# Four layers on a graph of 2048 nodes: adjacency loaded later, products ahead of the degrees, one-hot columns on ScalarE, 1/degree applied in the mixing

## The chip, the cores and the metric

The kernel runs on one core of a Trainium2 chip. Its engines are TensorE (PE: matmuls, with its weight loads listed apart as PEld), VectorE (DVE), ScalarE (ACT), GpSimd (POOL) and SyncE (SP, which only issues transfers here). Each engine works through its own queue in order; transfers are issued from the queues of SP, ACT and POOL. The metric is the device time of one execution in microseconds (us). A trace is one profiled execution; its span is counted from the first to the last instruction.

## The reference, cut to what matters

`x` is 8 x 2048 x 64, `adj` is 2048 x 2048 of zeros and ones with a full diagonal, `H` is 2048 x 64 (node by hyperedge). Four layers follow each other, each `x = layernorm(x + layer(x))`. The change touches layer 0:

```
h = x @ W                                    # 8 x 2048 x 64
alpha = softmax over the nodes of a hyperedge of leaky_relu(h @ a_node)
agg = alpha @ h                              # 8 x 64 hyperedges x 64
all_he[n, e] = elu(beta * h[n] + (1 - beta) * agg[e]),  beta = sigmoid(h[n] @ a_gn + agg[e] @ a_ge)
g[n] = sum over the hyperedges e of node n of softmax(scores of e) * all_he[n, e]
deg = max(sum of a row of adj, 1)
industry = (adj / deg) @ (x @ W_ind)
out = softmax-weighted mix of industry and g, by tanh(f @ fcW + fcb) @ av
```

Layers 1 to 3 are products with `adj` (layer 1 with 1/sqrt(deg + 1) on both sides), a Chebyshev convolution with node-wise weights, and three rounds of a small network on [v, adj @ v].

## The kernel before

The batch is worked in NP = 4 pairs (two batch entries of 64 features make 128 partitions). The nodes are NT = 16 tiles of 128 rows or NCH = 4 chunks of 512 columns; JT = 4 tiles make a chunk. The transposed adjacency stays in SBUF for the whole kernel as 16 tiles of 128 x 2048, 1 MB each, in a type with which a 128 x 512 matmul is fast; to keep precision every left operand is split into a high and a low part (`split`, L163), so that a product has two matmuls per tile and chunk. The names `ug`, `du`, `ph` and `pcm` are PSUM tiles that share one tag `ph` with two buffers of two banks.

The stages that the change touches, in order of time:

- **The loop over h** (L505 to L550), one iteration per node tile t. PE makes h for the four pairs (`ph`), DVE and ACT make a row block `st` of 584 columns per node (exponentials, (h+1) times e^gn, and the slot numbers of the node's hyperedges), which ACT's queue stores to `hs_hbm` (L538); PE also adds up `pagg`, the sums over the nodes of each hyperedge. `st` has four buffers. Adjacency tiles are loaded from POOL's queue by `load_adj` (L209): five ahead of the loop, each after a copy that waits for an x tile (`load_adj_after`, L395), ten more in the loop as `paced` says (L401), the last one after it. SP loads `xt` tiles four iterations ahead and, for the products, `xc` chunks, of which `parts` makes high and low parts (the low ones on POOL).
- **Hyperedges** (L572 to L639). `filler` is a generator of matmuls that `fill(n)` (L327) draws from: `products()` (L271). It first gives the 64 degree matmuls `du` (ones times an adjacency tile, 16 tiles x 4 chunks), then for each pair p and half g (two chunks of 512) the 64 matmuls of adj @ x in `ug`. Between the small steps of the hyperedge scores come fill(24), fill(14), fill(10) and fill(24): 72 of the 576 matmuls. From the degrees come `dinv` (for layer 1) and, by transposes, `inv` rows of 1/deg over all partitions, inside the first half. Each `ug` is multiplied by `inv` on DVE (L324) and stored to `u0_hbm` by SP.
- **The slot loop** (L693 to L724). The nodes are sorted by their number of hyperedges, so that tile t of the sorted order has 12, 5, 5, 4, 4, 4, 3, 3, 3, 3, 2, 2, 2, 2, 2, 1 slots (57 in all): slot s of a node is its s-th hyperedge. `fetch_rows` (L231) gathers the rows of a tile from `hs_hbm` by an indirect transfer on POOL's queue. `slots` (L241) makes from the slot numbers one-hot matrices `o`, 128 x 128, one per slot: by `is_equal`, on DVE for 8 of the first tile's and on POOL for the other 49. `begin` (L670) makes the high and low parts of a row block, and the coefficients R and co from the matmuls `ps` of o. For each slot PE adds three matmuls into `pz` (rows of h twice, and o times the hyperedge table), DVE multiplies by R, ACT takes the exponential into `y`, DVE makes the elu and multiplies by co, and POOL adds up `acc`. `pz` has three buffers, `y` two. Every slot draws fill(6), every tile but the last fill(3). The sums are scattered to `gs_hbm` from POOL's queue.
- **The mixing steps** (L867 to L891), 16 of them (pair by chunk), pipelined over two steps, with fills of eight matmuls in four places. `mix_parts` loads g and `u0_hbm`, multiplies by W_ind (`pi`) and copies the result into `ind`; `mix_scores`, `mix_weigh` and `mix_end` make the scores, the mix and the layernorm. The rest of `products()` is drawn in steps 0 to 4; from then on the filler is layer 1 (`layer1`, L830), whose operands `l1_parts` are made in step 4.

Matmuls and transposes made by `mm` and `transpose` (L172, L175) keep the order of the program, as do the adjacency loads and gathers on POOL and, for pair 0, the parts. A scheduler puts the other instructions into each engine's queue. Adjacency tile t and the parts' chunk t // 4 are needed by four matmuls in a half.

Of the kernel before, what the change touches and what calls it, by code (L numbers as in the profile page):

```python
# [37 lines left out]
ALU = mybir.AluOpType  # L38
# [18 lines left out]
def tile_gnn_fast(  # L57
# [47 lines left out]
    def cols(c, n=C):  # L105
        return slice(c * n, (c + 1) * n)
# [105 lines left out]


# [6 lines left out]
    x2_hbm = [dram.tile([P, NT, P], F32, name=f"x2_hbm{p}") for p in range(NP - 1)]  # L220
    gs_hbm = dram.tile([N, BF], F32, name="gs_hbm")
# [19 lines left out]
    def slots(t, psum, tag, bufs):  # L241

        pt = psum.tile([E, P], F32, tag=tag, name="pslot", bufs=bufs)
        transpose(pt, hrows[t][:, BF + 8:])
        slot = hy.tile([P, P], BF16, tag="slot", name="slot", bufs=2)
        for i in range(2):
            nc.scalar.copy(slot[i * E:(i + 1) * E, :], pt)
        one_hot[t] = []
        for s in range(sum(n > t for n in SLOT_TILES)):
            o = hrp.tile([P, P], F32R, tag="o", name="o", bufs=17)  # L250
            eng = nc.vector if t == 0 and s % 3 < 2 else nc.gpsimd
            made = eng.tensor_scalar(o, slot, float(s + 1), None, op0=ALU.is_equal)
            if t == 0:
                tc.keep_in_program_order(made)
            one_hot[t].append(o)
# [15 lines left out]
    def products():  # L271


        du = [pph.tile([P, 2, C], F32, tag="ph", name=f"du{g}", bufs=2) for g in range(2)]
        for t in range(NT):
            for c in range(NCH):
                mm(du[c // 2][:, c % 2, :], lhsT=ones_r, rhs=adj[t][:, cols(c)], start=t == 0, stop=t == NT - 1)
                yield
        for c in range(NCH):
            r = slice(c * P // NCH, (c + 1) * P // NCH)  # L280
            evacuate(deg4[r, :], du[c // 2][r, c % 2, :])
        deg1 = hy.tile([P, NT], F32, name="deg1")
        inv = []
        for p in range(NP):
            for g in range(2):
                own = (2 * g, 2 * g + 1)
                ug = pph.tile([P, 2, C], F32, tag="ph", name="ug", bufs=2)
                u = {c: ug[:, c % 2, :] for c in own}
                for t in range(NT):
                    for i in range(2):  # L290
                        for c in own:
                            mm(
                                u[c], lhsT=part[t // JT][i][:, t % JT, :], rhs=adj[t][:, cols(c)],
                                start=t == 0 and i == 0, stop=t == NT - 1 and i == 1,
                            )
# [7 lines left out]
                    if p == 0 and g == 0 and t == 3:  # L303

                        pdc = places["small"]([P, JT, P], "pdc")
                        for j in range(JT):
                            transpose(pdc[:, j, :], deg4[:, cols(j, P)])
                        pdc = pdc.rearrange("p j (c r) -> p c j r", c=NCH)[:, :, :, 0]
                        d1 = deg1.rearrange("p (c j) -> p c j", c=NCH)
                        nc.vector.tensor_scalar(d1, pdc, 1.0, None, op0=ALU.add)  # L310
                        nc.gpsimd.tensor_tensor(dinv, deg1, neg_half[:, :NT], ALU.pow)
                        nc.vector.tensor_scalar(d1, pdc, 1.0, None, op0=ALU.max)
                        nc.vector.reciprocal(deg1, deg1)
                    if p == 0 and g == 0 and t in (12, 13, 14, 15):
                        c = t - 12
                        pt = places["small"]([P, C], "pinv")
                        for j in range(JT):
                            k = c * JT + j
                            transpose(pt[:, cols(j, P)], deg1[:, k:k + 1].to_broadcast([P, P]))
                        inv.append(va.tile([P, C], F32, name=f"inv{c}"))  # L320
                        nc.scalar.copy(inv[c], pt)
# [14 lines left out]
    with tc.tile_pool(name="pa_ps", bufs=1, space=PSUM) as pps:  # L336
# [233 lines left out]
        ones_r = ta.tile([P, P], F32R, name="ones_r")  # L570
        nc.vector.tensor_copy(ones_r, ones)
# [19 lines left out]
        fill(14)  # L591
# [7 lines left out]
        fill(10)  # L599
# [37 lines left out]

        fill(NT * NCH - 48 + 8)
# [26 lines left out]
    with ExitStack() as pb_scope:  # L665
# [29 lines left out]
        for t in range(NT):  # L695
            S, both, ohs, R, co = now
            acc = pl.tile([P, B, F], F32, tag="acc", name="acc", bufs=2)
            for s in range(S):
# [6 lines left out]
                fill(6)  # L705
# [4 lines left out]
                y = pl.tile([P, B, F], F32, tag="y", name="y", bufs=2)  # L710
# [34 lines left out]
    mp = mix_scope.enter_context(tc.tile_pool(name="mix", bufs=1, side="right"))  # L745
    lps_scope = ExitStack()
# [7 lines left out]
    def mix_parts(i):  # L754

        p, c = divmod(i, NCH)
        gn = mp.tile([P, JT, P], F32, tag="gn", name="gn", bufs=2)
        nc.sync.dma_start(
            gn, gs_hbm[c * C:(c + 1) * C, p * P:(p + 1) * P].rearrange("(t p) f -> p t f", p=P)
        )  # L760
        ut = mp.tile([P, C], F32, tag="ut0", name="ut0", bufs=2)
        nc.sync.dma_start(ut, u0_hbm[p][:, cols(c)])
        pi = lps.tile([P, C], F32, tag="mm", name="pi", bufs=4)
        mm(pi, lhsT=bd_ind, rhs=ut, start=True, stop=True)
        inds[i] = mp.tile([P, C], F32, tag="ind", name="ind", bufs=2)
# [100 lines left out]

    steps = NP * NCH  # L867
# [1031 lines left out]
```

## Time and profile before

| what | value |
|---|---|
| three runs | 2235.95, 2239.82, 2240.61 us, median 2239.82 |
| the profiled run | 2242.28 us, span 2240.4 us |
| busy, share of the span | PE 88%, PEld 57%, DVE 50%, POOL 22%, ACT 17% |
| mean granted TensorE clock | 0.95 |
| loop over h, first matmul `ph` to last `pagg` | 21.1 to 79.8 us |
| degrees `du`, first to last | 79.8 to 98.1 us |
| slot loop, first `ps` to last matmul of its last slot | 100.7 to 279.3 us |
| first mixing matmul `pi` | 295.2 us |
| first matmul of layer 1 | 362.0 us |
| one-hot 128 x 128 on POOL, on DVE (medians) | 556 ns, 290 ns |
| landing of a 1 MB adjacency tile, of a 292 KB h store (medians) | 8.9 us, 6.3 us |

The page gives the whole execution in 40 slices of 56 us, each digit being a busy share in tenths; the stages of the table fill the first six and a half. Matmuls are pipelined, so that the time from one to the next is shorter than the duration that the trace gives for one.

### The profile page before, as it was taken

Reading aid. Unit: us, or ns where it says so; the run is one execution under the profiler, and the core shown is the slowest. Engines: PE = TensorE matmul, PEld = TensorE weight load, DVE = VectorE, ACT = ScalarE, POOL = GpSimd, SP = SyncE. Lnnn points to the kernel's source line nnn. Section 1 sums busy time; section 2 is a strip of 40 time slices with the busy share of each in tenths; the row PEclk is TensorE's granted clock in tenths of the full one; section 3 lists DMA queues with packets and bytes.
Section 4 is the critical chain, followed back from the end, with each engine's and each line's share of the span. In section 5 each row is a group of like instructions: output and inputs, shape, how many; then the busy total and the mean of one; then the engine's idle time right before and its main releaser. Section 6 shows DMA issues by size and latency. Waiting matters only on the chain. (4 is left out here: it accounts for less than half of the span.)

```text
span 2240.4 us, 19695 instructions
## 1 busy us (share of the span) xinstructions
PE 1981.7 (88%) x7292; PEld 1282.5 (57%) x7292; DVE 1110.8 (50%) x1837; ACT 376.2 (17%) x688; POOL 501.0 (22%) x464
## 2 busy tenths in 40 slices
PE   5898879998659999799999999999986998989994
PEld 3676645665544444375455456447444776867773
DVE  4478835666432232216854763782883233332322
ACT  1233323222111111110010001001001212212110
POOL 2378823344223232200110110100010010010102
PEclk8899989999869999999999999999998999999997
DMA  9612223222210000000000000000001101111110
GB/s 310 223 47 77 101 95 114 92 96 81 101 38 0 19 19 19 26 17 5 10 5 5 8 7 3 7 9 1 7 7 36 43 24 52 38 52 43 43 34 20
DMA packets 72521, 108.50 MB, mean 48 GB/s; under 512 B 26704, under 2 KB 34928, under 8 KB 69920
## 3 DMA queue, kind: packets, MB, share of 16 engines
q1 hardware_dynamic: 61728, 72.61, 10.5%
q0 software_dynamic: 5088, 25.89, 3.4%
q10 hardware_dynamic: 5600, 8.65, 1.1%
q8 instruction: 59, 0.97, 0.2%
q14 instruction: 46, 0.38, 0.1%
HBM read 78.22 MB, written 28.90 MB: 48 GB/s over the span
## 5 line engine op out<-in xcount | busy, mean ns | idle before, releaser
L1018 PE MATMUL py<-wp,xg 128*128 128x512 f32 x1024 | 448.4, 597 | 8.5 <-DVE fcav L1023 5.8
L1018 PEld LDWEIGHTS py<-wp,xg 128*128 128x128 f32 x1024 | 193.6, 191 | 254.3 <-issue 215.3
L173 PE MATMUL u<-adj,hi 128*128 128x512 f32 x768 | 255.8, 414 | 0.0
L173 PE MATMUL u<-adj,lo 128*128 128x512 f32 x768 | 247.4, 402 | 0.0
L965 PE MATMUL u<-pt,xn 128*128 128x512 f32 x512 | 230.6, 609 | 8.3 <-DVE u L974 7.1
L1023 DVE TENSOR_TENSOR fcav<-py,emb_n 128x512 f32<-128x512 f32 x256 | 177.1, 692 | 51.7 <-PE py L1018 37.1
L1024 DVE TENSOR_REDUCE r<-fcav 128x32 f32<-128x512 f32 x256 | 175.4, 685 | 8.1
L965 PEld LDWEIGHTS u<-pt,xn 128*128 128x128 f32 x512 | 98.5, 195 | 131.9 <-issue 117.0
L652 PE MATMUL u<-adj,vh 128*128 128x512 f32 x512 | 158.9, 409 | 15.1 <-ACT vh L168 11.0
L173 PEld LDWEIGHTS u<-adj,hi 128*128 128x128 f32 x768 | 142.9, 190 | 40.9 <-issue 11.2
L1026 POOL TENSOR_TENSOR r<-r,bias 128x256 f32<-128x256 f32 x32 | 23.4, 731 | 636.4 <-DVE r L1024 636.4
L173 PEld LDWEIGHTS u<-adj,lo 128*128 128x128 f32 x768 | 144.9, 190 | 33.8
L156 POOL TENSOR_TENSOR ln_r<-ln_e,neg_half 128x8 f32<-128x8 f32 x64 | 106.5, 1663 | 215.6 <-DVE ln_e L154 209.0
L652 PE MATMUL u<-adj,vl 128*128 128x512 f32 x512 | 152.3, 399 | 0.0
L959 DVE TENSOR_SCALAR pt<-pt 128x512 f32<-128x512 f32 x64 | 48.8, 780 | 175.0 <-ACT pt L958 173.4
L1114 DVE SCALAR_TENSOR_TENSOR fcav<-fcav,ar 128x512 f32<-128x512 f32 x64 | 44.3, 693 | 175.6 <-ACT ar L1113 175.4
L652 PEld LDWEIGHTS u<-adj,vh 128*128 128x128 f32 x512 | 96.4, 190 | 45.5 <-ACT vh L168 12.5
L1096 POOL TENSOR_TENSOR r<-r,xn 128x512 f32<-128x512 f32 x16 | 20.5, 1280 | 434.1 <-DVE r L1095 434.1
L963 POOL TENSOR_TENSOR acc<-acc,pt 128x512 f32<-128x512 f32 x60 | 79.7, 1328 | 165.6 <-DVE pt L959 162.7
L652 PEld LDWEIGHTS u<-adj,vl 128*128 128x128 f32 x512 | 96.7, 189 | 22.3 <-issue 0.7
L150 ACT ACTIVATE r<-ln_c 128x512 f32<-128x512 f32 x64 | 40.4, 631 | 270.4 <-DVE ln_c L146 255.6
L144 DVE TENSOR_REDUCE ln_m<-r 128x8 f32<-128x512 f32 x64 | 43.8, 685 | 70.0 <-POOL r L1030 27.9
(340 smaller groups left out, 2737.1 us busy)
## 6 DMA issues: line engine op xcount, KB each, us to landing
adj<-in_adj_t POOLq DMA_DIRECT2D x16, 1024.0 KB, 8.9
fcav<-in_adj_t SPq DMA_DIRECT2D x64, 256.0 KB, 2.9
x_hbm<-r SPq DMA_DIRECT2D x28, 256.0 KB, 2.1
hs_hbm<-st ACTq DMA_DIRECT2D x16, 292.0 KB, 6.3
xt<-in_x_t SPq DMA_DIRECT2D x16, 256.0 KB, 6.9
xc<-in_x_n SPq DMA_DIRECT2D x16, 256.0 KB, 2.7
u_hbm<-ut SPq DMA_DIRECT2D x16, 256.0 KB, 2.4
gn<-gs_hbm SPq DMA_DIRECT2D x16, 256.0 KB, 3.5
```

Of the source, the lines that this page charges most:

```text
L144: nc.vector.tensor_reduce(mean, r, AX.X, ALU.add)
L150: nc.scalar.activation(r, xc, AF.Square)
L156: nc.gpsimd.tensor_tensor(rstd, vare, neg_half[:, :groups], ALU.pow)
L173: tc.keep_in_program_order(nc.tensor.matmul(*args, **kw))
L652: nc.tensor.matmul(u[c], lhsT=half[:, j, :], rhs=adj[t][:, cols(c)], start=t == 0 and i == 0, stop=ends and not own,)
L959: nc.vector.tensor_scalar(pt, pt, 1.0, None, op0=ALU.max)
L963: nc.gpsimd.tensor_tensor(acc, acc, pt, ALU.add)
L965: nc.tensor.matmul(u[p], lhsT=xn[p][:, t, :], rhs=pt, start=t == 0, stop=t == NT - 1)
L1018: nc.tensor.matmul(py.rearrange("p o d -> p (o d)"), lhsT=xg[b][:, q, cols(j, P)], rhs=wp[:, q, cols(k)], start=q == 0, stop=q == 1,)
L1023: nc.vector.tensor_tensor(pr, py, e_b, ALU.mult)
L1024: nc.vector.tensor_reduce(r[:, j, b, cols(k, OH)], pr, AX.X, ALU.add)
L1114: nc.vector.scalar_tensor_tensor(a, a, 1.0, ar.bitcast(F32), op0=ALU.mult, op1=ALU.not_equal, accum_out=left[:, t, k:k + 1],)
```

## The change

- Three adjacency tiles instead of five are loaded ahead of the loop over h, five instead of ten in it (`paced`), and eight after it: one at once, and seven behind the gathers of the first two row blocks and the parts of the last two chunks.
- `products()` begins with the first half of pair 0; the 64 degree matmuls come after that half, two chunks at a time (`degrees`). What follows from the degrees (`inverses`) is spread over the second half of pair 0. ones_r is made at the start.
- The fills between the hyperedge steps are 10, 8, 8 and 6; each slot draws 7; 36 are drawn between the slot loop and the mixing. `y` has three buffers.
- The one-hots of the first tile are all made by DVE; the other 45 by ACT, in two activations: far = |slot - (s+1)|, o = relu(1 - far). The column `number` holds -(s+1).
- `ug` is copied by ACT without the factor 1/deg. The `inv` rows go to a buffer `inv_hbm` in memory, are loaded as one tile `inv_row` of 128 x 2048 when the mixing begins, and multiply `pi` where it was copied.

```diff
+    ones_r = hy.tile([P, P], F32R, name="ones_r")
+    nc.vector.tensor_copy(ones_r, ones)
+    number = hy.tile([P, 12], F32, name="number")
+    for i in range(12):
+        nc.gpsimd.memset(number[:, i:i + 1], -1.0 - i)
...
+    inv_hbm = dram.tile([P, N], F32, name="inv_hbm")
...
-            eng = nc.vector if t == 0 and s % 3 < 2 else nc.gpsimd
-            made = eng.tensor_scalar(o, slot, float(s + 1), None, op0=ALU.is_equal)
             if t == 0:
-                tc.keep_in_program_order(made)
+                tc.keep_in_program_order(
+                    nc.vector.tensor_scalar(o, slot, float(s + 1), None, op0=ALU.is_equal)
+                )
+            else:
+
+                far = hy.tile([P, P], BF16, tag="far", name="far", bufs=2)
+                nc.scalar.activation(far, slot, AF.Abs, bias=number[:, s:s + 1])
+                nc.scalar.activation(o, far, AF.Relu, bias=1.0, scale=-1.0)
...
-        du = [pph.tile([P, 2, C], F32, tag="ph", name=f"du{g}", bufs=2) for g in range(2)]
...
+        def degrees(g):
+            du = pph.tile([P, 2, C], F32, tag="ph", name=f"du{g}", bufs=2)
+            for t in range(NT):
+                for i in range(2):
+                    mm(
+                        du[:, i, :], lhsT=ones_r, rhs=adj[t][:, cols(2 * g + i)], start=t == 0, stop=t == NT - 1
+                    )
+                    yield
...
+                row = va.tile([P, C], F32, tag="ut", name="inv", bufs=2)
+                nc.scalar.copy(row, pt)
+                nc.sync.dma_start(inv_hbm[:, cols(c)], row)
...
+                turning = inverses() if p == 0 and g == 1 else iter(())
...
+                            if t > 1:
+                                next(turning, None)
...
-                    nc.vector.tensor_tensor(ut, u[c], inv[c], ALU.mult)
+                    nc.scalar.copy(ut, u[c])
                     nc.sync.dma_start(u0_hbm[p][:, cols(c)], ut)
+                if p == 0 and g == 0:
+                    yield from degrees(0)
+                    yield from degrees(1)
...
-        for t in range(5):
-            load_adj_after(t, xt[min(t, 3)][:, 0, 0:1])
-        paced = {1: 5, 2: 6, 4: 7, 5: 8, 7: 9, 8: 10, 10: 11, 11: 12, 13: 13, 14: 14}
+        for t in range(3):
+            load_adj_after(t, xt[t + 1][:, 0, 0:1])
+        paced = {2: 3, 5: 4, 8: 5, 11: 6, 14: 7}
...
-        load_adj(NT - 1)
+        load_adj(len(paced) + 3)
         fetch_rows(0)
         fetch_rows(1)
         for c in (2, 3):
             fetch(0, c)
             parts(0, c)
+        for t in range(len(paced) + 4, NT):
+            load_adj(t)
...
-        fill(24)
+        fill(10)
...
-        fill(14)
+        fill(8)
...
-        fill(10)
+        fill(8)
...
-        fill(NT * NCH - 48 + 8)
+        fill(6)
...
-                fill(6)
+                fill(7)
...
-                y = pl.tile([P, B, F], F32, tag="y", name="y", bufs=2)
+                y = pl.tile([P, B, F], F32, tag="y", name="y", bufs=3)
...
+    inv_row = mp.tile([P, N], F32, name="inv_row")
+    nc.scalar.dma_start(inv_row, inv_hbm[:])
...
-        nc.vector.tensor_copy(inds[i], pi)
+        nc.vector.tensor_tensor(inds[i], pi, inv_row[:, cols(c)], ALU.mult)
...
+    fill(36)
     steps = NP * NCH
```

More of the change, by code (lines that the diff above doesn't have):

```diff
@@ L271, in products, with inverses @@
     def products():
-        du = [pph.tile([P, 2, C], F32, tag="ph", name=f"du{g}", bufs=2) for g in range(2)]
-        for t in range(NT):
-            for c in range(NCH):
[L277 to L283, printed above, removed]
+        deg1 = hy.tile([P, NT], F32, name="deg1")
+        def degrees(g):
[6 more added lines that the diff above has]
+                    yield
+            for i in range(2):
+                c = 2 * g + i
+                r = slice(c * P // NCH, (c + 1) * P // NCH)
+                evacuate(deg4[r, :], du[r, i, :])
+        def inverses():
+            pdc = places["small"]([P, JT, P], "pdc")
+            for j in range(JT):
+                transpose(pdc[:, j, :], deg4[:, cols(j, P)])
+            pdc = pdc.rearrange("p j (c r) -> p c j r", c=NCH)[:, :, :, 0]
+            d1 = deg1.rearrange("p (c j) -> p c j", c=NCH)
+            nc.vector.tensor_scalar(d1, pdc, 1.0, None, op0=ALU.add)
+            nc.gpsimd.tensor_tensor(dinv, deg1, neg_half[:, :NT], ALU.pow)
+            nc.vector.tensor_scalar(d1, pdc, 1.0, None, op0=ALU.max)
+            nc.vector.reciprocal(deg1, deg1)
+            for _ in range(8):
+                yield
+            for c in range(NCH):
+                pt = places["small"]([P, C], "pinv")
+                for j in range(JT):
+                    k = c * JT + j
+                    transpose(pt[:, cols(j, P)], deg1[:, k:k + 1].to_broadcast([P, P]))
+                row = va.tile([P, C], F32, tag="ut", name="inv", bufs=2)
+                nc.scalar.copy(row, pt)
+                nc.sync.dma_start(inv_hbm[:, cols(c)], row)
+                for _ in range(4):
+                    yield
         for p in range(NP):
@@ L302, in products @@
                             fetch(p + 1, (c + 2) % NCH)
[L303 to L321, printed above, removed]
                 for c in own:
                     ut = va.tile([P, C], F32, tag="ut", name="ut", bufs=2)
-                    nc.vector.tensor_tensor(ut, u[c], inv[c], ALU.mult)
+                    nc.scalar.copy(ut, u[c])
                     nc.sync.dma_start(u0_hbm[p][:, cols(c)], ut)
+                if p == 0 and g == 0:
+                    yield from degrees(0)
+                    yield from degrees(1)
     def fill(n):
@@ L569, in tile_gnn_fast @@
         ta = ta_scope.enter_context(tc.tile_pool(name="ta", bufs=1, side="right"))
-        ones_r = ta.tile([P, P], F32R, name="ones_r")
-        nc.vector.tensor_copy(ones_r, ones)
         places["small"] = lambda shape, name: pps.tile(shape, F32, tag="sm", name=name, bufs=2)
         filler = products()
-        fill(24)
+        fill(10)
         gv = pagg[:, 0:G * (F + 1)].rearrange("p (g c) -> p g c", c=F + 1)
```

## The prediction, made before the changed kernel was run

> **What bounds the kernel now.** I read the page's slices first, to see where TensorE (PE) has gaps, then a table by stretch, then the chain of waits of the first 420 us, the groups by shape, and timelines at the joints. All sums are against the profiled span, 2240.4 us; the three other runs have a median of 2239.8.
>
> ```profile
> PE   5898879998659999799999999999986998989994
> POOL 2378823344223232200110110100010010010102
> PEclk8899989999869999999999999999998999999997
> GB/s 310 223 47 77 101 95 114 92 96 81 101 38 0 19 19 19 26 17 5 10 5 5 8 7 3 7 9 1 7 7 36 43 24 52 38 52 43 43 34 20
> ```
>
> Slices are 56 us. PE is near full after 350 us, short of it in slices 1 to 6, and the DMA engines are busy at the start. All edits but the mixing's act before 362 us, so I cut that part at its joints. The columns are PE, PEld, VectorE (DVE), ScalarE (ACT), GpSimd (POOL) busy us with counts, PE clock, DMA share, GB/s:
>
> ```profile
> 16.40:79.80 63.40, 46.44 (x244) 31.41 (x244) 35.46 (x123) 10.95 (x51) 10.15 (x23) 0.78 0.96 342
> 79.80:100.70 20.90, 19.99 (x88) 16.10 (x87) 7.83 (x27) 7.24 (x19) 8.44 (x10) 0.94 0.46 157
> 100.70:117.80 17.10, 16.05 (x72) 12.84 (x71) 8.37 (x21) 2.31 (x5) 8.98 (x9) 0.90 0.10 32
> 117.80:279.30 161.50, 138.49 (x582) 106.15 (x580) 130.83 (x225) 54.06 (x111) 137.51 (x132) 0.96 0.24 77
> 279.30:295.20 15.90, 0.00 (x0) 0.01 (x1) 5.74 (x7) 0.60 (x1) 4.35 (x4) 0.64 0.34 123
> 295.20:361.90 66.70, 63.59 (x225) 40.49 (x225) 34.64 (x47) 22.83 (x35) 17.87 (x13) 0.96 0.32 101
> ```
>
> Row 1 is the loop over h: DMA share 0.96. Row 2 is the hyperedge part with the degrees; rows 3 and 4 the slot loop (its sixth slot starts at 117.8); row 5 a hole without one matmul; row 6 the mixing steps up to layer 1's first product. In row 4 POOL (137.5), PE (138.5) and DVE (130.8) are all within 20% of 161.5: three engines coupled, POOL with the most to lose.
>
> ```profile
> ACT st L520 <- DMA hs_hbm<-st: 29.9, 9, 7.5
> PE pi L173 <- DMA ut<-u_hbm: 15.9, 1, 15.9
> PEld ps L173 <- POOL o L252: 13.6, 15, 2.9
> PE ps L173 <- POOL o L252: 10.4, 14, 2.7
> ...
> L719 POOL TENSOR_TENSOR acc<-acc,y 128x512 f32<-128x512 f32 x41 | 54.3, 1325 | 20.8 <-DVE y L718 16.8 <-DVE R L685 2.1 <-DVE R L682 0.7
> L718 DVE TENSOR_TENSOR y<-y,co 128x512 f32<-128x512 f32 x41 | 42.6, 1050 | 0.1
> L252 POOL TENSOR_SCALAR o<-slot 128x128 fp32r<-128x128 bf16 x46 | 28.9, 639 | 3.5 <-ACT slot L247 2.6
> ```
>
> The four waits name the four places: rows of h that can't leave (29.9), the hole (15.9), one-hots that come late from POOL (10.4 on PE; the 13.6 of the weight loads is largely the same time). The groups show what POOL does there.
>
> ```profile
> 113.84 0.39 PE L173 MATMUL pz<-hrh,ident_r 128*128 128x512 f32 x1
> 115.92 0.39 PE L173 MATMUL pz<-hrh,ident_r 128*128 128x512 f32 x1
> ...
> 349.32 1.02 PE L173 MATMUL pi<-ut,bd_ind 128*128 128x512 f32 x2
> 357.35 1.02 PE L173 MATMUL pi<-ut,bd_ind 128*128 128x512 f32 x2
> ```
>
> An undisturbed slot of 3+6 matmuls takes 2.08 us, 0.23 each. A mixing step that has only five product matmuls left takes 8.0 us; one with 32 takes 14.3 (320.7 to 335.0).
>
> **What the Trainium skill says.** "DMA: Bandwidth & Descriptors", section "Issuing engines are not separate DMA queues": transfers from ACT, SP and GpSimd run on the same 16 engines and interleave. The trace agrees: the 292 KB h stores, on another queue than adjacency, take 6.3 us (median) while 1 MB tiles pass. "GPSIMD Engine Reference", section "Key points": it shares SBUF interfaces with VectorE and collides with VectorE instructions of two SBUF inputs. The trace agrees: y*co averages 1050 ns here, and 0.68 us where POOL rests. "ScalarE: Activation LUTs", section "Table sets": relu and abs are in every set. The trace has one table load, at 11.7 us, for exp and tanh; abs and relu are not in it.
>
> **The change, part by part.** PE work is moved, not removed: 64 degree and 512 product matmuls stay. The fills before the slot loop fall from 72 to 32, those inside rise from 387 to 444, 36 come behind it, and 64 are left for the mixing instead of 117. The order on each engine below is that of the built program.
>
> 1. *The loop over h.* It moved 342 GB/s x 63.4 us = 21.7 MB. About 7.7 adjacency tiles leave it, 8.1 MB; 13.6 MB at the same rate take 40 us, so it would end at 56. Undisturbed, an iteration takes 1.8 us (38.3 to 45.6 for four); the first three, mixed with the sort, lasted to 33.8; 13 x 1.8 and the last sum give 59. Some store waits stay: I take 62 for 79.8. The twelve extra memsets on POOL at the start cost what the sixteen of `caps` do, under 0.6 us, before a transfer-bound stretch: nothing on the path.
>
> 2. *To the slot loop.* ps started 20.9 us after the loop. Now only 24+8 matmuls stand between the small steps (he, pht, tanh, pse, slots) instead of 64+8; the row gather waits for the last h store (10.1 us now; I take 5), then 2 us of issue and 3.6 to land, slot copies 0.5, twelve one-hots on DVE 2.2 (8 took 1.45). I take 14 us: ps at 76.
>
> 3. *Tiles 9 to 15.* They stand on POOL's queue behind those gathers and the low parts v2l and v3l, so issue starts about 10 us after the loop. Seven tiles of 1.05 MB at 370 GB/s (between the 342 mean and the peaks above 400) and 2 us give the last at +32. PE waits in order: pz and ps stand behind the product that needs the tile. The sixth slot starts some 14 matmuls later: 62+32+3 = 97 instead of 117.8. Gained 21, with 35 matmuls (8 us) deferred.
>
> 4. *Rest of the slot loop, 52 slots.* PE: 52x10+14x3 = 562 matmuls x 0.23 = 130, plus ps, transposes, pinv about 11: 141, at a clock of 0.97 145; the same sum for now (510) gives 134 at 0.96, so 27 of 161.5 are lost. POOL loses 45 one-hots, about 28 us, and DVE the multiply by 1/degree (12 x 0.67) and some collisions. ACT gets 45 pairs. The row for far is missing; the nearest, tanh with a column bias, takes 475 ns at 256 and 684 at 512 elements: 371 at 128; casts give 298. The skill's price (same page, "What ACT_TABLE_LOAD costs") is 387 and 293, less 93 overlap each. So 0.5 to 0.67 us a pair, 22 to 30 us, and 0.58 for each ut copy: ACT goes from 54 to about 88 of 160. In order on ACT, exponentials stand behind a batch of up to five pairs, 2.5 us; three pz and now three y buffers cover about 6 us of slots. I take the one-hot waits as gone and 14 us of the 27 as left: 159. Slot loop ends at 256 instead of 279.3: 23. The degrees' PSUM tiles share two buffers with the products; ut's copies stand behind four exponentials, with three slots of slack: no cost, at most 2.
>
> 5. *The hole* stays 16 us, but 36 matmuls (8.3) run in it, which pays for most of what was deferred.
>
> 6. *Mixing until layer 1.* Steps of 11.1, 14.3, 10.6 (16 fills), 8, 8 = 52 instead of 62: 10. Layer 1's first product waits 3.15 for v0h now; the casts stand earlier in the new order: 1 to 3 more. I take 11. The product with inv_row replaces a PSUM copy of the same shape (0.68): nothing. Its 1 MB load stands on ACT's queue and may wait for the last scatter, as gn does; it lands 7 to 9 us later, ind(0) was due about 5 after: 0 to 5 lost, I take 3; behind it on ACT only two ut copies that nobody needs yet. Four 256 KB stores of inv pass where DMA moves 77 GB/s: nothing.
>
> Sum: 23+11-3 = 31. 2240 - 31 = **2209 us**. After 362 us nothing changes.
>
> **Rivals.**
> (a) *VectorE takes over in the slot loop.* DVE is busy 130.8 of 161.5 with two SBUF inputs beside POOL's acc. If the 27 us of loss stay, the stretch takes 172: gain 31-13, 2222. Against: POOL's share falls by a fifth.
> (b) *The h loop isn't released.* If store latency, not bytes, holds it, it still ends near 79, 17 worse: 2226. For: a store is waited for 7.5 us; against: share 0.96 at 342 GB/s.
> (c) *Slower: ACT's queue.* The one-hot batch of every tile delays the exponentials, and PE stalls on pz. Fourteen batches of 2.5 to 3 us, wholly exposed, cost up to 42: 2251. It decides from 2.2 us exposed a batch. Against: ACT is idle 107 of 161 us and three pz are ahead.
> (d) *Better.* All losses of the slot loop but 5 us go and the loop ends at 58: 2196 or below.
>
> **How the numbers follow.** A measurement tells 0.2%, 4.5 us, from no change. Forecast (own range 2198 to 2219) 0.53; (a) 0.17; (b) 0.10; (d) 0.09; within 0.2% by mixtures of (a), (b) and late tiles 0.04; (c) 0.07. Faster 0.53+0.17+0.10+0.09 = 0.89. The range 2190 to 2231 holds forecast, (a), (b) and most of (d).
>
> **What would show it.** Right: last pagg near 62, store waits under 12 us; PE waiting for adj near 85 to 95; no PE wait on one-hots above 3 us in total; slot loop ending near 256; the hole half filled; pi to pi of 8 us from the fourth step. Wrong: a loop that ends after 75, ACT waits in front of pz, or a slot loop over 170 us behind its sixth slot.

## The result and the profile after

| | before | after |
|---|---|---|
| median of the runs | 2240.2 us (2236.0 to 2242.5) | 2217.2 us (2212.4 to 2221.3) |
| ratio, 95% interval | 1 | 0.990 [0.987, 0.993] |
| profiled run: span, PE clock | 2240.4 us, 0.950 | 2213.6 us, 0.952 |
| profiled run: layer 1's first product | 361.96 us | 337.28 us |

The changed kernel is 23 us faster by the medians; the forecast was 31. Of the 26.8 us between the two profiled spans 24.7 lie ahead of layer 1's first product. The slices of the page, 55 us each:

```profile
PE   5799889898849999799999999999896999989994
...
POOL 2368623434223333100100110110110010110102
PEclk8799989999869999999999999999998999999997
GB/s 261 278 78 100 114 108 109 93 99 63 114 12 0 19 19 19 43 1 8 8 5 5 10 5 3 8 10 0 10 5 42 39 26 56 39 52 39 47 30 21
```

The first two GB/s entries, 310 and 223 before, are 261 and 278: traffic went from the first slice into the second, and the first 110 us moved about the same sum. POOL's third to fifth digits, 7 8 8 before, are 6 8 6: the slot loop without its one-hots. The table by stretch, with the columns of the prediction, says it more plainly:

```profile
14.40:75.00 60.60, 42.46 (x245) 28.36 (x245) 35.96 (x122) 11.69 (x52) 6.55 (x13) 0.81 0.82 277
75.00:86.80 11.80, 11.41 (x50) 9.09 (x48) 4.80 (x20) 4.66 (x15) 7.16 (x9) 0.84 0.42 114
86.80:110.50 23.70, 19.93 (x70) 15.01 (x71) 14.09 (x32) 6.97 (x20) 8.60 (x9) 0.78 0.87 337
110.50:261.70 151.20, 142.31 (x638) 113.21 (x638) 131.41 (x215) 80.22 (x203) 117.17 (x90) 0.99 0.29 94
261.70:278.30 16.60, 8.60 (x37) 6.56 (x35) 3.08 (x5) 1.67 (x3) 3.37 (x3) 0.85 0.42 151
278.30:337.20 58.90, 53.54 (x171) 31.51 (x172) 28.71 (x38) 21.15 (x34) 17.53 (x12) 0.90 0.32 102
```

Row 1, the loop over h, moves 277 GB/s where it moved 342, and is hardly shorter: 60.6 us against 63.4. Row 4, from the sixth slot on, is the large gain: 151.2 us against 161.5, with 56 more matmuls in it, POOL at 117 instead of 137 us and PE idle for 8.9 instead of 23.0. Row 5 is the hole, now with 36 products in it. The waits of the first 340 us that answer to those shown of before (us in total, times, longest):

```profile
ACT st L547 <- DMA hs_hbm<-st: 18.3, 8, 6.6
...
POOL hrow L240 <- DMA hs_hbm<-st: 13.2, 1, 13.2
...
PE pi L173 <- DMA ut<-u_hbm: 8.1, 1, 8.1
...
PE pt L176 <- DVE ind L824: 5.3, 1, 5.3
...
PE ug L173 <- DMA adj<-in_adj_t: 3.2, 4, 1.3
...
PE ps L173 <- ACT o L265: 0.6, 1, 0.6
```

Rows of h still wait for their stores. The wait in the hole has halved. A product waits for an adjacency tile four times, 3.2 us. PE waits 0.6 us for one-hots where it waited 10.4. The groups of the slot loop (busy us, mean ns, then idle time before them):

```profile
L745 POOL TENSOR_TENSOR acc<-acc,y 128x512 f32<-128x512 f32 x41 | 55.5, 1354 | 35.9 <-DVE y L744 33.3 <-DVE R L711 2.0
L744 DVE TENSOR_TENSOR y<-y,co 128x512 f32<-128x512 f32 x41 | 48.9, 1206 | 0.3
...
L264 ACT ACTIVATE far<-slot,number 128x128 bf16<-128x128 bf16 x45 | 15.8, 391 | 0.3
L265 ACT ACTIVATE o<-far 128x128 fp32r<-128x128 bf16 x45 | 11.5, 296 | 0.0
```

A one-hot on ScalarE is 391 and 296 ns; an estimate by the price in the Trainium skill, "ScalarE: Activation LUTs", section "What ACT_TABLE_LOAD costs", is 387 and 293 (280 or 186 ns and 0.833 ns an element). There is still one table load, 1.28 us at 11.2, so abs and relu cost no second one, as its section "Table sets" has it. VectorE's product beside POOL's sum did not get cheaper: 1206 ns, before 1050. There are still collisions, but from the sixth slot to the last PE no longer waits for y (2.9 us before). The joints of the mixing:

```profile
278.36 2.04 PE L173 MATMUL pi<-ut,bd_ind 128*128 128x512 f32 x2 [8.06 <-DMA ut<-u_hbm]
...
314.27 1.02 PE L173 MATMUL pi<-ut,bd_ind 128*128 128x512 f32 x2
327.08 1.91 PE L173 MATMUL pi<-ut,bd_ind 128*128 128x512 f32 x2
336.07 1.02 PE L173 MATMUL pi<-ut,bd_ind 128*128 128x512 f32 x2
```

The fourth step takes 12.8 us and the fifth 9.0, where 8 were forecast for each.

### The profile page after: what moved, and what is told of

It is laid out like the page before. It is cut to its first block, busy times and chain, and to the rows that moved or that the text cites. A ratio compares the mean times of both kernels' runs of the same rounds, so it can differ in the third digit from the quotient of the medians.

```text
span 2213.6 us, 19723 instructions
## 1 busy us (share of the span) xinstructions
PE 1972.6 (89%) x7292; PEld 1277.5 (58%) x7292; DVE 1112.3 (50%) x1825; ACT 405.9 (18%) x794; POOL 474.8 (21%) x420
## 5 line engine op out<-in xcount | busy, mean ns | idle before, releaser
L173 PEld LDWEIGHTS u<-adj,hi 128*128 128x128 f32 x768 | 143.4, 190 | 40.9 <-issue 11.2
L1143 ACT CAST ar<-fcav 128x512 fp32r<-128x512 f32 x64 | 39.7, 621 | 213.8 <-DMA fcav<-in_adj_t 144.8
```

Source lines behind the costliest of these rows:

```text
L173: tc.keep_in_program_order(nc.tensor.matmul(*args, **kw))
L1143: nc.scalar.copy(ar, a)
```

## The experiments

Every profile was cut at the same joints: the first h product (ph), the loop over h from its first sum to the end of its last, the sixth slot, the last slot, the first mixing product (pi) and layer 1's first product. All in us, from one profile each but for the last column:

| kernel | loop over h | ph to 6th slot | 6th to last slot | last slot to pi | pi to layer 1 | ph to layer 1 | median, ratio to before |
|---|---|---|---|---|---|---|---|
| before | 51.4 | 96.9 | 159.0 | 18.2 | 66.7 | 340.8 | 2240.2 |
| after | 49.4 | 91.7 | 148.6 | 18.9 | 58.9 | 318.2 | 2217.2, 0.990 [0.987, 0.993] |
| no tiles in the loop | 41.4 | 93.8 | 148.8 | 19.3 | 59.1 | 321.0 | 2219.9, 0.990 [0.988, 0.992] |
| eight row buffers | 42.2 | 91.1 | 149.2 | 18.8 | 59.1 | 318.2 | 2217.9, 0.990 [0.987, 0.992] |
| old order of tiles | 50.6 | 90.6 | 148.4 | 19.3 | 58.0 | 316.3 | 2221.7, 0.991 [0.988, 0.994] |
| three tiles early | 45.8 | 83.4 | 149.5 | 18.9 | 58.8 | 310.6 | 2209.5, 0.986 [0.984, 0.988] |
| one-hots on GpSimd | 46.2 | 94.2 | 167.2 | 19.1 | 57.8 | 338.2 | 2234.0, 0.998 [0.997, 0.999] |
| before, one-hots on ScalarE | 51.2 | 98.3 | 147.0 | 15.6 | 66.1 | 327.0 | 2229.6, 0.995 [0.994, 0.996] |
| no products in the hole | 46.7 | 94.3 | 148.9 | 18.3 | 62.5 | 324.0 | 2220.1, 0.991 [0.989, 0.993] |
| products spread | 43.0 | 91.2 | 149.1 | 19.1 | 55.7 | 315.1 | 2212.4, 0.989 [0.987, 0.991] |
| two y buffers | 47.2 | 94.2 | 151.4 | 18.9 | 59.4 | 324.0 | 2222.5, 0.992 [0.990, 0.995] |
| early, spread | 47.5 | 86.1 | 150.1 | 19.5 | 53.3 | 309.0 | 2204.3, 0.984 [0.982, 0.985] |
| early, 70 in the hole | 45.6 | 84.1 | 148.5 | 18.7 | 51.3 | 302.7 | 2201.4, 0.982 [0.981, 0.984] |
| the same, eight buffers | 42.5 | 87.3 | 150.3 | 19.1 | 49.6 | 306.4 | 2202.8, 0.984 [0.982, 0.986] |

How far a cell can be trusted shows in the kernels that are the same up to that joint. After, no products in the hole, products spread and two y buffers have one and the same loop over h, and it took 49.4, 46.7, 43.0 and 47.2 us (mean 46.6); ph to the sixth slot 91.7, 94.3, 91.2 and 94.2 (mean 92.9). A difference of 3 us ahead of the sixth slot means nothing in a single profile. The first h product itself stood at 19.1 us in the profile of after and at 20.8 to 22.6 in all the others; it is no part of the gain. The stretches behind the sixth slot repeat within about 2 us. What follows layer 1's first product, which no edit touches, varied from 1870 to 1882 us, so that a few us of a median can come from there as well. Each ratio is to runs of the kernel before on the same chip, whose medians were 2238.3 to 2241.6.

The 22.6 us that the change gained up to layer 1's first product lie at 5.2 ahead of the sixth slot (4.0 with the mean of the four), 10.4 in the slot loop and 7.8 in the mixing; the hole took 0.8 more.

### What ends the loop over h

**No tiles in the loop.** The rest of the kernel is as changed.

```diff
-        paced = {2: 3, 5: 4, 8: 5, 11: 6, 14: 7}
+        paced = {}
```

> The changed kernel, with its five adjacency tiles inside the loop over h moved behind it (three ahead of the loop stay, thirteen follow). Bytes theory: 5.2 MB less in the loop, so it ends near 59 (1.8 us an iteration) instead of 75.0. Store-return theory (a row buffer is free only when the store of four iterations before has landed, and stores land late only while 1 MB tiles are on their way): the same 59, with the waits for stores under 3 us instead of 18.3. A third theory, that vector work or the sort holds the loop: it still ends at 72 or later. After it thirteen tiles need 37 us at 370 GB/s and about 10 to start, so the last lands near 106, as now: products wait longer for tiles (over 8 us instead of 3.2), and the whole is 2212 to 2222.

The loop took 41.4 us and ended at 69.4, not 59; 3 us of that are its later start. Nearly all the bytes in dispute are gone (the one tile that follows the loop in the program is asked for at 54.2 here and lands 9.5 us later, still inside it), and 1.8 us an iteration still isn't reached. Waits for stores are left:

```profile
ACT st L547 <- DMA hs_hbm<-st: 12.8, 6, 5.8
PE ug L173 <- DMA adj<-in_adj_t: 10.6, 7, 6.8
```

Both theories that promised 59 are wrong by 7 us and more; the third, which said 72 or later, is nearest and missed too. What the loop saves comes back as products that wait for tiles (10.6 us, over 8 were expected), and the whole, 2219.9, is in the range given.

**Eight row buffers.** Bytes and tiles as changed.

```diff
-            st = pa.tile([P, HROW], F32, tag="st", name="st", bufs=4)
+            st = pa.tile([P, HROW], F32, tag="st", name="st", bufs=8)
```

> The changed kernel with eight row buffers st for h instead of four; the bytes and the tiles stay as they are. Store-return theory: the 18.3 us of waits for stores fall below 4, and the loop over h ends between 62 and 68 instead of 75.0; the whole is 2206 to 2213. Bytes theory: the loop still ends at 73 to 76, since the same megabytes have to pass, and the wait moves to the x tiles or to the end of the loop; the whole is within 4 us of 2217.

```profile
ACT st L547 <- DMA hs_hbm<-st: 9.1, 4, 5.0
```

The loop took 42.2 us, as short as with no tiles at all, though every byte still passed: eight buffers alone are worth about 4 us against the mean of the four same loops (46.6). So bytes alone don't hold it (a second kernel with eight buffers, the last of the table, took 42.5). The waits only halved (9.1, not under 4) and it ended at 70.8, 3 us above what was expected, as it began 3 us later: the row buffers are a good part of it, not the whole. The whole, 2217.9, fits the other theory and not the 2206 to 2213 of this one. Nothing was gained in the end: ph to the sixth slot is 91.1.

**Old order of tiles.** Five ahead, ten inside, one behind.

```diff
-        for t in range(3):
-            load_adj_after(t, xt[t + 1][:, 0, 0:1])
-        paced = {2: 3, 5: 4, 8: 5, 11: 6, 14: 7}
+        for t in range(5):
+            load_adj_after(t, xt[min(t, 3)][:, 0, 0:1])
+        paced = {1: 5, 2: 6, 4: 7, 5: 8, 7: 9, 8: 10, 10: 11, 11: 12, 13: 13, 14: 14}
```

> The changed kernel with the old order of adjacency tiles: five ahead of the loop over h, ten inside, one behind. All other edits stay. If the tiles' move is worth only what the loop's end shows, first slots at about 79.8 + 12 = 92 instead of 86.8 but no product waits for a tile (3.2 us, and the slow start of the sixth slot, given back): within 4 us of 2217. If the move of the tiles is what carries the gain (18 of 31 us in the prediction), 2228 to 2235.

The loop is as long as before (50.6), and no product waits for a tile; the sixth slot comes 90.6 us behind the first h product, with the new order 91.7. The median, 2221.7, lies just outside the range of the first theory and 6 us under that of the second, and the intervals of the two ratios nearly coincide. **Moving the tiles out of the loop is worth nothing that these runs can tell**: about 4 us of loop, all given back.

**Three tiles early.** As many tiles in the loop as changed, other places.

```diff
-        paced = {2: 3, 5: 4, 8: 5, 11: 6, 14: 7}
+        paced = {6: 6, 11: 7}
...
         nc.vector.tensor_tensor(slot, pcm, m_n, ALU.mult)
+        for t in (3, 4, 5):
+            load_adj_after(t, slot[:, 0, 0:1])
...
-        load_adj(len(paced) + 3)
+        load_adj(8)
...
-        for t in range(len(paced) + 4, NT):
+        for t in range(9, NT):
```

> The changed kernel with the same number of tiles ahead of and inside the loop over h, but three of the five inside it are started at about 20 us, as soon as the slot numbers are there, instead of behind iterations 2, 5 and 8; the other two behind iterations 6 and 11. From 20 to 35 us the DMA engines moved only 108 to 134 GB/s in the changed kernel. Theory that idle transfer time early and a crowd of tiles late make the loop end at 75: it ends at 62 to 68, store waits under 10 us, the whole 2207 to 2213. Bytes theory without regard to the place: 73 to 76, the whole within 4 us of 2217. Third: early tiles delay the first stores instead, and the loop ends at 75 or later.

POOL's timeline shows what the places are. First after, then early tiles (start, duration, what the engine waited for):

```profile
31.65 0.18 POOL L423 COPY seen_x<-seen 128x1 f32<-128x1 f32 x1 [19.09 <-DVE lr L551]
32.10 0.54 POOL L211 DMA_DIRECT2D adj<-in_adj_t  x1 [0.27 <-issue]
...
65.07 1.06 POOL L211 DMA_DIRECT2D adj<-in_adj_t  x2 [0.27 <-issue]
79.31 1.06 POOL L240 DMA_INDIRECT hrow<-hs_hbm,order  x1 [13.17 <-DMA hs_hbm<-st]
...
84.15 3.92 POOL L211 DMA_DIRECT2D adj<-in_adj_t  x7
```

```profile
22.61 0.18 POOL L423 CAST seen_x<-slot 128x1 f32<-128x1 bf16 x1 [8.70 <-DVE fcav L525]
23.06 0.53 POOL L211 DMA_DIRECT2D adj<-in_adj_t  x1 [0.26 <-issue]
...
59.49 1.10 POOL L211 DMA_DIRECT2D adj<-in_adj_t  x2 [0.27 <-issue]
74.43 1.06 POOL L240 DMA_INDIRECT hrow<-hs_hbm,order  x1 [13.84 <-DMA hs_hbm<-st]
```

In after the third iteration's tile is asked for at 32 us, while the transfers of 20 to 35 us ran at 121 GB/s (292 with early tiles); the last two start at 65, 5 to 8 us ahead of the last three rows, with early tiles 8 to 12 us ahead of them. Those three stores land in 5.0 to 6.8 us in after (up to 9.6 in the three others of its kind), and in 2.1 to 4.1 in the three kernels with early tiles and four buffers. The row gather, which needs the last of them, starts 60.2 us behind ph in after (58.8 to 64.2 in its like) and 53.7 to 55.8 in those three.

The whole, 2209.5, is in the range of the first theory, but its mechanism was wrong: the loop ends at 72.9, not at 62 to 68 (45.8 us of loop is within the spread), and the waits for stores are 23.3 us, where under 10 were expected. The gain is there all the same, behind the loop: 8.3 us at the sixth slot (the means of three and of four kernels, 84.5 and 92.9), 7.7 in the median, with intervals of the ratios that barely overlap.

The next stage doesn't wait for the loop's last sum. It waits for a chain that begins when the **last store lands**: the row gather, and behind it on POOL's queue the seven last tiles (84.15 in the first timeline). From the gather's start to the landing of the last of them it is 26.5 to 28.1 us in all ten kernels with seven tiles there, and the sixth slot starts 3.1 to 4.8 us later, since the products of the last tile stand ahead of it on PE:

```profile
106.18 1.22 PE L173 MATMUL ug<-adj,v3h 128*128 128x512 f32 x2 [1.35 <-DMA adj<-in_adj_t]
```

The kernel without tiles in the loop shows that the store counts only through this chain. Its last store lands early, the gather starts 49.0 us behind ph, 11 us earlier than in after, and the sixth slot comes no earlier (93.8), because twelve tiles stand behind the gather, and the last of them, asked for at 90.5, lands 89.1 us behind ph:

```profile
70.77 1.06 POOL L240 DMA_INDIRECT hrow<-hs_hbm,order  x1 [15.98 <-DVE tab L630]
...
75.60 4.34 POOL L211 DMA_DIRECT2D adj<-in_adj_t  x8
...
90.53 0.57 POOL L211 DMA_DIRECT2D adj<-in_adj_t  x1 [2.29 <-DMA adj<-in_adj_t]
```

With the old order of tiles none stands behind the gather, but it starts only 67.4 us behind ph.

### What the slot loop gained from

**One-hots on GpSimd**, all else as changed.

```diff
-                far = hy.tile([P, P], BF16, tag="far", name="far", bufs=2)
-                nc.scalar.activation(far, slot, AF.Abs, bias=number[:, s:s + 1])
-                nc.scalar.activation(o, far, AF.Relu, bias=1.0, scale=-1.0)
+                nc.gpsimd.tensor_scalar(o, slot, float(s + 1), None, op0=ALU.is_equal)
```

> The changed kernel with its 45 one-hot columns of tiles 1 to 15 made by GpSimd again (is_equal), all else as changed. Theory that GpSimd's relief is what shortened the slot loop: from the sixth slot to the last 156 to 161 us instead of 148.6 (159.0 in the kernel before), PE waits for one-hots of 8 us or more, the whole 2224 to 2230. Rival: the third y buffer, the product by 1/degree gone from VectorE and seven products a slot did it: the stretch stays within 2 us of 148.6 and the whole within 4 of 2217.

**One-hots on ScalarE in the kernel before**, the same edit the other way round, alone.

> The kernel before with one edit: the one-hot columns of tiles 1 to 15 come from ScalarE (abs and relu), those of tile 0 as before. Theory that GpSimd's relief carries the slot loop's gain: from the sixth slot to the last 148 to 152 us instead of 159.0, the waits of PE for one-hots gone (10.4 before), the whole 2229 to 2234. Rival: alone it does little, because VectorE and the two y buffers hold the loop: over 155 us, the whole 2236 to 2241. Rival slower: exponentials stand behind the one-hots on ScalarE: over 161, 2243 or more.

The stretch from the sixth slot to the last, in four kernels (before; one-hots on ScalarE alone; after; after with one-hots on GpSimd):

```profile
118.00:277.00 159.00, 136.00 (x572) 104.47 (x571) 128.37 (x219) 52.78 (x109) 135.44 (x129) 0.96 0.24 78
```

```profile
120.88:267.90 147.02, 130.67 (x573) 101.22 (x572) 134.11 (x221) 73.33 (x190) 113.58 (x91) 0.99 0.27 84
```

```profile
110.79:259.40 148.61, 139.72 (x627) 111.13 (x626) 129.78 (x212) 79.33 (x201) 116.05 (x89) 0.99 0.29 94
```

```profile
116.06:283.20 167.14, 147.78 (x627) 115.82 (x626) 141.43 (x212) 59.14 (x121) 138.71 (x131) 0.95 0.26 83
```

With one-hots on ScalarE the stretch is 147 to 149 us, without them 159 and 167. The edit is worth 12.0 us alone and 18.6 in the changed kernel, where 7 to 12 were expected; the medians say 9.3 alone and 16.8. So the theory's sign is right and its size too small: the stretch of 167 and the whole, 2234.0, lie above the ranges given for the first run, and the 147.0 of the second lies just below its 148. In the kernel with one-hots on GpSimd PE waits 5.5 us for them, less than the 8 expected, and 7.7 for y.

Two things stand in the last row. PE's same 627 matmuls are 8.1 us longer, at a granted clock of 0.95 instead of 0.99. An estimate from the two rows: 0.05 of 167 us against 0.01 of 149 is 7 us of clock not granted, most of the 8.1. The Trainium skill, "TensorE: Matmul & The Clock Gate", section "Part 1: The HAM clock gate", has it that the clock is gated by how busy PE has been recently. The four rows agree only roughly: the two at 0.99 have 3.9 and 4.2 matmuls a us, those at 0.95 and 0.96 have 3.8 and 3.6, but PE is idle for 11% of the second row and for 12% of the fourth, so that the sum of idle time alone doesn't tell the clock. And VectorE is 11.7 us longer: its y*co averages 1457 ns there, beside a POOL that runs 138.7 of 167 us.

Alone on the kernel before, the edit gives four tenths of the whole gain; without it only 5 of the 23 us are left. The rest of the change makes use of it: 54 more matmuls pass in 148.6 us than in 147.0.

**Two y buffers.** `bufs=3` is `bufs=2` again for y.

> The changed kernel with two y buffers instead of three, all else as changed. If the one-hot batches on ScalarE need the third buffer as slack for the exponentials behind them: from the sixth slot to the last 153 us or more instead of 148.6, with PE waiting for pz, the whole 2221 or more. If they don't, as the kernel before with ScalarE's one-hots and two buffers suggests (147.0 there with one product fewer a slot): 148 to 150, the whole within 4 us of 2217.

151.4 us, between what the two theories said; PE then waits once for y (0.9 us). The stretch is 2.8 us longer, at the edge of what one profile tells, and the granted clock in it is 0.98 instead of 0.99, by which 1.5 us of the 2.8 can be explained (an estimate, 0.01 of 151). The whole, 2222.5, isn't told from 2217 by its interval. That the third buffer is worth anything is not shown.

### The hole and the mixing

**No products in the hole.** The line `fill(36)` is gone.

> The changed kernel without the 36 products put into the hole between the slot loop and the mixing; they run in the mixing steps 2 to 4 instead. Forecast's theory: the first mixing product starts at the same place (about 16.6 us after the slot loop's end), PE is idle 16 us there instead of 8.1; the mixing takes 36 x 0.23 = 8.3 us more, less what now fills the 5.3 us wait of its fourth step: 61 to 66 instead of 57.7 from the first pi to the sixth, the whole 2220 to 2225. Rival: the mixing is bound by its chain of small steps and hides them: within 2 us of 2217.

PE waited 15.8 us in the hole, as expected; the mixing took not 61 to 66 but 58.1 us from the first pi to the sixth (57.7 in after), and to layer 1's first product it was 62.5, 3.6 us more than in after. The 36 products of 0.23 us are worth 3.6 there (2.9 from the last slot on), not 8.3: the mixing has room for most of them. In the medians it is 3 us, within the intervals; the whole, 2220.1, is just inside the forecast's range, by less work than it supposed.

**Products spread.**

```diff
-        k = 10 if i > NCH else 8
+        k = 10 if i > NCH else 4
```

> The changed kernel with the 64 products left for the mixing spread thinner: 4 at each place of the first five steps instead of 8, so that they last into the fifth step. If the 12.8 us of the fourth step (5.3 us of PE waiting for VectorE) come from having nothing to fill it with: steps near 9, 10.6, 10.6, 10.6, 9, in all 50 to 54 from the first pi to the sixth instead of 57.7, the whole 2211 to 2215. If the chain of VectorE and GpSimd in that step is longer than the products: still 56 or more, the whole within 3 us of 2217.

```profile
281.52 2.05 PE L173 MATMUL pi<-ut,bd_ind 128*128 128x512 f32 x2 [8.23 <-DMA ut<-u_hbm]
290.60 1.02 PE L173 MATMUL pi<-ut,bd_ind 128*128 128x512 f32 x2
301.19 1.02 PE L173 MATMUL pi<-ut,bd_ind 128*128 128x512 f32 x2
311.79 1.02 PE L173 MATMUL pi<-ut,bd_ind 128*128 128x512 f32 x2
322.38 1.02 PE L173 MATMUL pi<-ut,bd_ind 128*128 128x512 f32 x2
331.12 1.02 PE L173 MATMUL pi<-ut,bd_ind 128*128 128x512 f32 x2
```

Steps of 9.1, 10.6, 10.6, 10.6 and 8.7 us, 49.6 in all, 8.1 less than in after. Layer 1's first product then waits 4.6 us for its left operand, so 3.2 are left at that joint. The ratios' intervals overlap (0.989 and 0.990); the joints tell the two apart. What the fourth step of after waited for stands in its timeline:

```profile
320.60 2.01 POOL L156 TENSOR_TENSOR ln_r<-ln_e,neg_half 128x8 f32<-128x8 f32 x1 [4.52 <-DVE ln_e L154]
322.58 2.92 POOL L811 TENSOR_TENSOR t<-t,t 128x512 f32<-128x512 f32 x2
322.64 1.74 DVE L157 TENSOR_TENSOR r<-ln_c,ln_r 128x512 f32<-128x512 f32 x1 [1.53 <-POOL ln_r L156]
324.31 1.75 DVE L824 SCALAR_TENSOR_TENSOR ind<-ind,gt 128x512 f32<-128x512 f32 x1
325.98 0.68 DVE L822 TENSOR_TENSOR ind<-ind,gt 128x512 f32<-128x512 f32 x1
...
326.20 1.09 PE L176 MATMUL pt<-ident,ind 128*128 128x128 f32 x4 [5.30 <-DVE ind L824]
```

`ind` (line 824) stands on VectorE behind a layer norm's last product, which waits 1.53 us for POOL's power; then POOL subtracts twice, and both VectorE instructions take 1.75 us; the same shape takes 0.68 as soon as POOL rests (line 822). With products left, PE is busy meanwhile.

**Together.** Early tiles and spread products:

> The changed kernel with two edits that each helped alone: three of the loop's tiles started at about 20 us, and 4 products at each place of the first five mixing steps instead of 8. If their gains stand in different places they add: 7.7 + 3 to 5 under 2217, so 2204 to 2207, a first slot near 86 and 54 to 56 us from the first pi to layer 1. If one takes what the other took: 2208 to 2212.

2204.3 us, the sixth slot 86.1 us behind ph and 53.3 from pi to layer 1: the gains add, as they stand in different places (the first slot, expected near 86, came at 88.7). Early tiles, 70 products in the hole and 2 at each mixing place:

```diff
-    fill(36)
+    fill(70)
...
-        k = 10 if i > NCH else 8
+        k = 10 if i > NCH else 2
```

> The same early tiles, with 70 products in the hole behind the slot loop instead of 36 and 2 at each mixing place instead of 8. The hole has 8.1 us of PE idle left, room for 35 products of 0.23. If the first mixing product still comes about 19 us behind the last slot, the hole's idle time falls below 2 us. PE's sum for the mixing is 5 steps of 6.9 us and 30 products, 41 us; if the small steps' chain allows it: 44 to 50 us from the first pi to layer 1 instead of 58.9, the whole 2198 to 2203. If that chain is the bound, as the run without the 36 products suggests: 52 us or more, the whole 2204 to 2209.

```profile
254.74:273.44 18.70, 18.70 (x82) 14.84 (x80) 4.57 (x8) 2.27 (x4) 4.46 (x4) 1.00 0.41 141
273.44:324.78 51.34, 43.77 (x139) 23.36 (x138) 33.56 (x43) 22.95 (x37) 19.03 (x13) 0.94 0.39 124
```

PE is never idle in the hole (18.70 of 18.70). The mixing takes 51.3 us, between what the two theories said, with PE idle for 7.6 of them: with 30 products left the chain of small steps shows. At **2201.4 us, 0.982 [0.981, 0.984]** this is the fastest kernel of the study, 16 us under the changed one and below its interval. From early and spread to this one the medians differ by less than their intervals. Of the 6.3 us between them from ph to layer 1 only 2.8 lie behind the last slot, where the two kernels differ; the rest is the spread of single profiles.

> The one with early tiles and 70 products in the hole, with eight row buffers for h as well. Alone the buffers shortened the loop over h from 49.4 to 42.2 us and gave nothing in the end, because the row gather still waits for the last store. If that holds here too: within 3 us of the one with four buffers. If with early tiles the bus is free at the loop's end and the last store lands earlier: 3 to 6 us less.

Eight buffers shorten the loop here too (42.5) and give nothing again: 2202.8. The loop's end moves, the last store doesn't land earlier (the gather starts 56.6 us behind ph, without them 54.1).

## Why the prediction was right, and where it was not

2209 was forecast, with 2190 to 2231; 2217 came. Two terms of the sum were mis-sized, in opposite directions: the loop over h ended 13 us later than forecast, and the slot loop was 8 us shorter. That the total came as near as 8 us is in part luck. Against the profiled run:

| step | forecast | measured |
|---|---|---|
| 1. loop over h ends | 62 | 75.0 |
| 2. from there to the first ps | 14 | 11.8 |
| 3. from the loop's end to the sixth slot | 35 | 35.8 |
| 4. rest of the slot loop | 159 | 151 |
| 5. the hole | 16, half filled | 16.6, 8.1 idle |
| 6. pi to layer 1 | 66.7 - 11 + 3 = 59 | 58.9 |

- **Step 1 failed**: it priced 8.1 MB at 342 GB/s, 24 us, and took 18. Set against the same kernel with the old order of tiles, their move shortens the loop by about 4 us (50.6 to a mean of 46.6), and the sixth slot comes no earlier. A DMA share of 0.96 said that the engines were busy, not that each megabyte costs its transfer time: with the five tiles gone the loop still takes 41.4 us, and eight buffers do the same with the five tiles there. This is rival (b), and only half of it was seen: a store's way back holds the loop in part, but what the next stage needs is the last store, and the tiles queued behind it. What else makes the loop longer than 16 times 1.8 us with the five tiles gone stays open; its first iterations run between pieces of the sort, which no run changed.
- **Step 3** names the right thing, the last tile, and the wait for tiles came where it was put: the last tile is used at 106.2, 31 us behind the loop's end, after four waits of 0.6 to 1.4 us. Its length is less sure than the table shows: in the three kernels that are the same up to there the sixth slot comes 39 to 42 us behind the loop's end, as it hangs on the tiles behind the gather and not on that end.
- **Step 4 was too cautious by 8 us**: 14 of 27 us of loss were kept, 8.9 of PE's idle time are left. The part on POOL was right (28.9 us of one-hots gone), the part on VectorE wrong: collisions stayed, at 1206 ns, and didn't matter. Rival (a) needed them to matter. Rival (c), exponentials behind batches of one-hots, shows as 0.6 us on PE, and as at most 2.8 us when the third y buffer is taken away.
- **Step 5**: the hole is as forecast, its worth was not: about 3 us for 36 products, because the mixing could hide most of them.
- **Step 6** is right by errors that cancel. The steps took 57.7 us from the first pi to the sixth instead of 52: the 8.0 us that a step of before took with five products did not carry over to the fourth step of after (12.8), in which VectorE's instructions stand beside POOL's. inv_row cost nothing, 3 were set: its issue waits 8.5 us behind the last scatter on ScalarE, as supposed, but lands before `ind` asks. And layer 1's wait shrank by 3.4 us (from 4.6 to 1.2 behind the sixth pi).
- Of the signs named, the half-filled hole and one-hot waits under 3 us (0.6) came. The loop's end (75.0, the very limit named for being wrong), the store waits (18.3, not under 12), the tile waits (at 98 to 106, not 85 to 95), the slot loop's end (261.7, not 256) and steps of 8 us did not.
- The moved fills alone, with neither the tiles' order nor the one-hots, were not run; that they bring the first slot 5 us nearer to the loop's end is read from the kernel with the old order of tiles (16.0 us, before 20.9). The factor 1/degree in the mixing was not run alone either.

## What to carry to other kernels

Before a megabyte taken out of a stage is priced at its transfer time, look for the one thing that the next stage waits for. Here that was a chain: the landing of one small store, a gather that needs it, and seven tiles queued behind the gather. Moving seven tiles behind it gave nothing, and starting three others 9 to 21 us earlier, in a gap of the traffic, gave 8 us. An engine that is 85% busy in a loop coupled with two others is worth relieving even if its partner's instructions get no cheaper: 45 small instructions of 0.64 us were worth 12 us alone and 19 in a denser loop. Filler products belong where small dependent instructions leave PE idle, and in such steps they cost less than their own time: 36 of them moved out of the mixing into an idle hole were worth about 3 us, not their 8.3.

## What was not expected of the hardware

That a slower stretch can cost twice on PE. The same 627 matmuls took 139.7 us where PE is idle for 8.9 us (clock 0.99), and 147.8 where it is idle for 19.4 (0.95): of the 18.6 us that the one-hots cost in the changed kernel 8.1 are in the matmuls' own time. What lowers the clock is not shown: the kernel before with one-hots on ScalarE is idle for 16.4 us and keeps 0.99.

And how much the price of a collision moves. VectorE's product beside POOL's sum, a shape that takes 0.68 us where POOL rests, was 1050 ns on average before, 1206 in the shorter loop of the changed kernel and 1457 in the longest. So the price does not follow the length of the loop. The Trainium skill, "SBUF — State Buffer", section "SBUF: two separate sides", calls the pair of ports that the two share an exclusive lock, held for the whole instruction; the 1.74 and 1.75 us beside POOL's two subtractions (1.46 each) in the mixing agree roughly with one instruction that waits for another.
